# One iteration of an attention loop in another TensorE order: next queries unbroken, the last score block behind them, one projection moved

## The chip, the cores and the metric

The kernel runs on one core of one Trainium2 chip. Its five engines each work through a queue of their own: TensorE (PE, matrix products; its weight loads are listed as PEld), VectorE (DVE), ScalarE (ACT), GpSimd (POOL) and SyncE (SP, which here only issues DMA transfers). The metric is the time of one execution on the device in microseconds (us), and less is better.

## The reference

The kernel computes `x + ffn(attention(x))` in float32 with these steps:

- Attention over 16 sequences of 512 tokens with 512 features, 16 query heads of 64 features, and one key head and one value head that all query heads share. The input is normalised per token; `q = xn @ Wq / 8` and `k, v = xn @ Wkv`. The scores get a bias per head (given, 512 x 512), a causal mask and a mask of invalid keys, and one extra "null" key and value that every query may see. Softmax, the value product, an output product `out @ Wo` and a second normalisation follow.
- A routed feed-forward layer: an RMS norm, a router over 16 experts, the top 512 of 8192 tokens for each expert, two matrix products with a GELU between them, a share of each expert's result by its gate, and a scatter-add to the tokens.

Cut to the part that the change touches:

```
sim  = einsum('bhid,bjd->bhij', q, k) + bias      # scores
sim  = where(causal or masked, -big, sim)
attn = softmax(sim)
out  = einsum('bhij,bjd->bhid', attn, v)          # value product
out  = layernorm(out @ Wo) * g_out                # projection
```

## The kernel before, in words

The program has three stages: attention, the choice of tokens, and the experts. The change touches attention only.

**Tiling.** The loop `for p in range(B * HP + 1)` (L714) runs over pairs of heads: `B` = 16 sequences times `HP` = 8 pairs. `b` is the sequence and `hp` the pair in it. The 512 queries of a sequence are four blocks of 128. For causality block `q` needs only the first 128 * (q + 1) keys, so the four score blocks of one head are 128, 256, 384 and 512 columns wide.

**Software pipeline.** Four pairs are in work in one iteration. `now` is the pair whose scores are made and reduced. `ahead` is the next pair, whose queries are projected. `behind` is the pair before `now`: its probabilities are turned by DVE in 32 x 32 squares (`turn`, tile `sq`), and 16 DMAs (`move`: 10 issued by SP and 6 by POOL) put the squares in place (tile `pt`). `turned` is the pair before that, whose value product is made (`attend`, tile `ap`, copied by ACT to a tile `ot`, of which each sequence has 8). Beside these, the loop projects the sequence before with `Wo` (`second`, tile `op`) in the iterations hp = 1 to 7: a sequence has 8 pieces, 4 tiles of 128 tokens times 2 halves of the columns, and each piece is a sum over the 8 tiles `ot`, made in two steps of four products. It also normalises tiles of the sequence before (`OutNorm`) and of the sequence two ahead (`InNorm`), turns the next sequence's inputs (tile `xtp`, in `first`, hp = 0 to 3) and makes its keys and values (`kvs`, tile `kp`, hp = 2 and 4 in most sequences).

**What sets the order.** The order on each engine is the order in which the Python code calls it; nothing reorders it (`Pinned`, L121 to L138). The helpers `steps` and `some` split the generators: `queries()` stops after two of its four products, and `project()` stops after four of its eight. Each float32 product is two records of the profile.

**Products on PE.** Queries (`qp`), projection (`op`), keys and values (`kp`) and turns (`xtp`) use the array as a whole (128 rows by 128 columns in the profile's form "128*128"). Scores (`sp`) contract over 64 features and use the array's two row halves side by side ("64*128"); a bfloat16 product with `one_sb` (`sp<-km,one_sb`) puts the mask of keys in place first. The value product (`ap`) has 64 output columns per head and uses the two column halves side by side ("128*64").

**Buffers that tie the engines.** Score tiles have four PSUM buffers. `scores(3)` takes two, `scores(2, 0)` two, and `scores(1)` takes again the two that `scores(3)` had, so that it waits until DVE has reduced block 3 (`reduce`, which writes the minimum `nm`). The tile `sq` has one buffer: DVE may turn the next pair only when all 16 DMAs that read it have landed. PSUM tiles of queries, projection and value product rotate through three buffers (`ps_m`).

**Waits inside an iteration.** On DVE: reduce blocks 3, 2, 0; turn `behind`; what is left of the norms of the iteration before (`late`); reduce block 1; the first step of this iteration's norm (`n.a()`); sums; the second step (`n.b()`), which waits for a power that POOL computes (`lo_r`) in its queue behind its six DMA issues. On ACT: exponentials, the copy of the queries (`qa`), exponentials of block 1, the exponential of the null key (`ne`), the copy `ot`, then the normalising products. In iteration hp = 1 the projection needs, in its very last product, the eighth `ot` of the sequence before, which the same iteration's `attend` makes.

Of the kernel before, what the change touches and what calls it, by code (L numbers as in the profile page):

```python
# [26 lines left out]
def tile_adaln_ffn(  # L27
# [113 lines left out]
    with ExitStack() as st:  # L141
# [75 lines left out]
        def load_turned(hp):  # L217

            w = work.tile([P, DC, P], F32, name=f"wot_{hp}", tag="z" if hp % 4 < 2 else "xf")
            sy.dma_start(out=w, in_=wo_tc[:, :, hp * P : (hp + 1) * P])  # L220
            wots[hp] = w
# [17 lines left out]
        def router_column(hp):  # L239

            w = wots.pop(hp)
            wp = ps_m.tile([P, E], F32, name=f"wp_{hp}", tag="m")
            for c in range(DC):
                te.matmul(wp, w[:, c, :], rw_sb[:, c, :], start=(c == 0), stop=(c == DC - 1))
            se.copy(wo_sb[:, hp, D:], wp)
# [42 lines left out]
        def load_bias(p):  # L288

            b, hp = divmod(p, HP)  # L290
            bt = biasp.tile([P, 2, SW], F32, name=f"bias_{p}", tag="bias")
            sy.dma_start(out=bt, in_=causal[hp] if b > kept_in(hp) else bias[hp])
            return bt
# [5 lines left out]
        def mask_bias(p, bt):  # L299

            b, hp = divmod(p, HP)
            if b > kept_in(hp):
                return
            with tc.issue_after(ge.last.ins):
                for q in range(QB):
                    diag = bt[:, :, off[q] + ext[q] - P : off[q] + ext[q]]
                    ge.affine_select(
                        out=diag, in_=diag, pattern=[[0, 2], [-1, P]],
                        compare_op=ALU.is_ge, fill=-BIG, base=0, channel_multiplier=1,
                    )  # L310
            if b == kept_in(hp):
                ge.dma_start(out=causal[hp], in_=bt)
# [326 lines left out]
        def steps(*parts):  # L639
            for part in parts:  # L640
                if hasattr(part, "__next__"):
                    yield from part
                else:
                    part()
                yield

        def some(todo, n=None):

            while n is None or n > 0:
                if next(todo, todo) is todo:  # L650
                    return
                n = None if n is None else n - 1
# [39 lines left out]
        for pair in ((0, 1), (2, 3)):  # L692
            begun = [InNorm(seqs[0], t) for t in pair]
# [19 lines left out]
        now, behind, turned, late = None, None, None, ()  # L713
        for p in range(B * HP + 1):  # L714
            b, hp = divmod(p, HP)
            now, ahead = ahead, None
            if p + 1 < B * HP:
                if p > 0:
                    biases[p + 1] = load_bias(p + 1)
                ahead = Pair(seqs[(p + 1) // HP], (p + 1) % HP)  # L720
            bt = biases.pop(p, None)
            chains = [InNorm(seqs[c], t) for c, t in ins.get(p, ())]
            if p in norms:
                chains.append(OutNorm(seqs[norms[p][0]], norms[p][1]))
            second = steps(*[seqs[c].project(*divmod(h, 2)) for c, h in halves.get(p, ())])
            asked = ahead.queries() if ahead else steps()

            if now:
                now.scores(3)
                now.scores(2, 0)  # L730
                now.reduce(3, bt)
                now.exps(3)
                now.reduce(2, bt)
                now.reduce(0, bt)
                now.exps(2)
                now.exps(0)
            for n in late:
                n.root()
            if now and behind:
                behind.turn()  # L740
                behind.move(sy, range(6, SN * SN))
                behind.move(ge, range(6))
            for to, what in later.get(p, ()):
                sy.dma_start(out=to, in_=what)
            if 0 <= p - 2 < HP:
                load_turned(p - 2)
            if 0 <= p - HP < NT // P:
                rows = slice((p - HP) * P, (p - HP + 1) * P)
                sy.dma_start(out=out_t[rows, :], in_=x_t[rows, :])
            for c, t in loads.get(p, ()):  # L750
                seqs[c].load(t)
            for n in late:
                n.d()
                if isinstance(n, OutNorm):
                    n.route()
            some(asked, 1)
            if now:
                now.scores(1)
            else:
                seqs[end].project_part(2, range(early))  # L760
                behind.turn_last()
                seqs[end].project_part(3, range(early))
            some(asked)
            if now:
                now.reduce(1, bt)
                now.exps(1)
            some(second, 1)
            for n in chains:
                n.a()
            if p == 3:  # L770
                some(centered, 1)
            if now:
                now.sums()
            for part in kvs.get(p, ()):
                part()
            if p == 3:
                some(centered, 1)
            for c in {4: (0, 1)}.get(p, (p - 3,) if 4 < p < 3 + HP else ()):
                router_column(c)
            if turned:  # L780
                turned.attend()
            for n in chains:
                n.b()
            if p == 3:
                some(centered)
            if p + 1 < B * HP:
                mask_bias(p + 1, biases[p + 1])
            if now:
                now.normalize(0)
                now.normalize(3)  # L790
            for part in first.get(p, ()):
                part()
            if now:
                now.normalize(2, 1)
            some(second, 2)
            some(second)
            for n in chains:
                n.c()
            late = chains
            if HP - 2 <= p - end * HP < HP:  # L800
                seqs[end].project_part(p - end * HP - HP + 2, range(early))
            if not now:
                behind.attend()
            turned, behind = behind, now
# [505 lines left out]
    now = Expert(0, first)  # L1310
# [11 lines left out]
    for e in range(E):  # L1322
# [24 lines left out]
        if e == 0:  # L1347
# [10 lines left out]
            late = [part[3] for part in t]  # L1358
        else:
# [9 lines left out]
            late = []  # L1369
# [27 lines left out]
        now = nxt  # L1397
# [61 lines left out]
```

## Time and profile before

| what | value |
| --- | --- |
| median of 3 runs | 3511.76 us |
| lowest and highest | 3511.39 and 3514.19 us |
| the profiled execution's own time | 3511.39 us |
| its span (first to last instruction) | 3509.5 us |
| attention stage, roughly | 0 to 1840 us |
| choice of tokens | 1840 to 1990 us |
| experts | 1990 to 3509.5 us |
| PE busy in 500 to 1800 us | 1283.5 of 1300 us |

How to read it: the profile lists each engine's busy time, the granted TensorE clock in tenths, and the chain of work that ended last. A PE that reads busy is not one at its peak: the end of each product is modelled and overlaps the next product's start. What one product costs is therefore read from the distance between two starts. Attention takes about 110 us for each sequence in its steady part: the projections' long rows in the chain of waits repeat at 1001.14, 1110.77, 1223.99, 1334.09, 1443.09 and 1552.48 us.

### The profile page before, as it was taken

How to read it: one execution, taken by the hardware profiler on the slowest of the kernel's cores; microseconds unless marked ns; L12 is line 12 of the kernel's file. 1: busy time of each engine (PE TensorE's matmuls, PEld its weight loads, DVE VectorE, ACT ScalarE, POOL GpSimd, SP SyncE). 2: the span in 40 equal slices, each digit the busy share in tenths (PEclk: the TensorE clock that was granted, in tenths of full speed). 3: DMA queues.
4: the chain of work that ended last, by engine and by line, in shares of the span. 5: the costliest groups of instructions: out<-in, count | busy, mean ns of one | idle time of the engine just before them, and what ended most of it. 6: DMA issues, size and time to landing. Idle time of an engine off the chain costs nothing.

```text
span 3509.5 us, 50838 instructions
## 1 busy us (share of the span) xinstructions
PE 3352.9 (96%) x16100; PEld 2366.1 (67%) x16100; DVE 2342.2 (67%) x6089; ACT 1555.0 (44%) x4100; POOL 922.2 (26%) x1375
## 2 busy tenths in 40 slices
PE   7999999999999999999991899999999999999999
PEld 3555555555555555555550788888888888888887
DVE  6677777777777777776658865556556656655553
ACT  5676676677776777767640221111111211211111
POOL 3343333333333333333320222222111211222110
PEclk9999999999999999999995899999999999999999
DMA  6887877777776667667633244444333444444430
GB/s 218 272 254 241 254 227 230 219 242 229 231 233 204 209 216 216 207 209 214 197 112 110 83 144 129 134 127 127 107 102 122 139 135 131 132 127 127 135 101 12
DMA packets 272194, 601.33 MB, mean 171 GB/s; under 512 B 53032, under 2 KB 126424, under 8 KB 253496
## 3 DMA queue, kind: packets, MB, share of 16 engines
q1 hardware_dynamic: 213744, 467.72, 40.4%
q0 software_dynamic: 44272, 111.78, 13.5%
q10 hardware_dynamic: 13911, 18.60, 2.1%
q8 instruction: 129, 2.11, 0.2%
q14 instruction: 138, 1.12, 0.1%
HBM read 368.52 MB, written 61.87 MB: 123 GB/s over the span
## 4 chain that ended last, share of the span: by engine, by line
PE 81%; DVE 6%; issue 1%; SPq 1%; POOL 1%; DMA 1%; ACT 0%; DVEq 0%; POOLq 0%
PE op L131 11%; PE qp L131 10%; PE r_y L131 9%; PE sp L131 8%; PE pc L131 6%; PE pc_y L131 6%; PE pa_y L131 6%; PE pa L131 6%; PE ap L131 6%; PE pe L131 3%; PE pb L131 3%; PE pd L131 3%; DVE sq L131 2%; PE kp L131 1%; DVE p L131 1%
## 5 line engine op out<-in xcount | busy, mean ns | idle before, releaser
L131 DVE CUSTOM_DVE_ANT_0 p<-sp,bias,nn_sb 128x512 f32<-128x512 f32 (+3 forms) x1024 | 500.1, 544 | 256.8 <-PE sp L131 230.5
L131 ACT ACTIVATE p<-p,nm 128x512 f32<-128x512 f32 (+3 forms) x1024 | 561.8, 550 | 187.9 <-DVE nm L131 186.6
L131 POOL DMA_DIRECT2D pt<-sq x762 | 382.4, 508 | 840.8 <-issue 497.9
L131 PE MATMUL qp<-xnt,wq_sb 128*128 128x512 f32 x1024 | 514.7, 626 | 0.0
L131 PE MATMUL op<-wo_sb,ot 128*128 128x272 f32 (+1 forms) x1920 | 470.9, 391 | 4.3 <-ACT ot L131 4.3
L131 PEld LDWEIGHTS op<-wo_sb,ot 128*128 128x128 f32 x1920 | 357.8, 191 | 116.4 <-issue 55.0
L131 DVE STREAM_TRANSPOSE sq<-p 128x896 f32<-128x896 f32 x762 | 398.5, 587 | 24.1 <-DMA pt<-sq 10.1
L131 POOL DMA_INDIRECT out_dram<-y,tok x64 | 106.2, 1660 | 1151.7 <-ACT y L1278 1130.4
L131 ACT ACTIVATE p<-p,rs 128x512 f32<-128x512 f32 (+2 forms) x768 | 402.8, 603 | 1.3 <-DVE rs L131 1.3
L1186 ACT ACTIVATE h<-h,b_sb 128x512 f32<-128x512 f32 (+1 forms) x256 | 143.4, 607 | 526.6 <-DVE h L131 467.0
L131 PE MATMUL sp<-ka,qa 64*128 64x512 f32 (+3 forms) x2048 | 357.6, 440 | 1.6 <-ACT qa L131 1.6
L1278 ACT ACTIVATE y<-y,gg 128x512 f32<-128x512 f32 x64 | 46.2, 722 | 609.6 <-DVE y L131 411.1
L131 PE MATMUL ap<-pt,vp 128*64 128x512 f32 (+3 forms) x2048 | 310.1, 446 | 2.2 <-DMA x<-in_x_dram 1.2
L131 PEld LDWEIGHTS qp<-xnt,wq_sb 128*128 128x128 f32 x1024 | 175.4, 191 | 183.3 <-issue 167.8
L131 PEld LDWEIGHTS ap<-pt,vp 128*64 128x64 f32 x2048 | 138.0, 138 | 191.7 <-issue 159.6
L131 PE MATMUL pa<-xe,w 128*128 128x256 f32 x1024 | 243.6, 381 | 0.0
L131 PEld LDWEIGHTS sp<-ka,qa 64*128 64x128 f32 x2048 | 174.5, 190 | 86.0 <-issue 80.1
L131 PE MATMUL pa_y<-w,h 128*128 128x256 f32 x1024 | 231.5, 379 | 0.0
L131 PE MATMUL r_y<-w2t,hs 128*128 128x256 f32 x1024 | 231.5, 379 | 0.0
L131 PEld LDWEIGHTS pa<-xe,w 128*128 128x128 f32 x1024 | 195.6, 191 | 26.8
L131 PEld LDWEIGHTS r_y<-w2t,hs 128*128 128x128 f32 x1024 | 194.6, 190 | 26.5
L131 PEld LDWEIGHTS pa_y<-w,h 128*128 128x128 f32 x1024 | 194.6, 190 | 26.5
(201 smaller groups left out, 4959.5 us busy)
## 6 DMA issues: line engine op xcount, KB each, us to landing
bias<-causal SPq DMA_DIRECT2D x108, 1280.0 KB
w<-in_fc_dram SPq DMA_DIRECT2D x256, 512.0 KB
pt<-sq SPq DMA_DIRECT2D x1270, 80.0 KB
pt<-sq POOLq DMA_DIRECT2D x762, 80.0 KB
bias<-in_bias_dram SPq DMA_DIRECT2D x20, 1280.0 KB
x<-in_x_dram SPq DMA_DIRECT2D x64, 256.0 KB
out_dram<-in_x_dram SPq DMA_DIRECT2D x64, 256.0 KB
table<-xf SPq DMA_DIRECT2D x64, 256.0 KB
```

Source lines behind the costliest of these rows:

```text
L131: self.last = tc.keep_in_program_order(made(*args, **kwargs))
L1186: nc.scalar.activation(a[0], a[1], AF.Gelu, bias=b1_sb[:, self.e, f : f + 1])
L1278: nc.scalar.activation(y, y, AF.Copy, scale=self.gg[:, g, self.e : self.e + 1])
```

## The change

The loop's body is put in another order, in four points.

- The next pair's four query products stand in a row. Before, block 1's scores stood in the middle of them.
- Block 1's scores, and their reduction and exponentials, come behind the queries and behind the first half of the first projection piece. That first half (`some(second, 1)`) now stands ahead of the scores.
- In iterations hp = 1 that first half is not made there at all: the whole projection stands behind the value product.
- Where the iteration before left no norms (`late` is empty), the first step of this iteration's norms comes ahead of block 1. Otherwise it stays behind it.

No product, copy or transfer is added or removed.

```diff
-            some(asked, 1)
+            some(asked)
+
+            if hp != 1:
+                some(second, 1)
+            begun = () if late else chains
+            for n in begun:
+                n.a()
             if now:
                 now.scores(1)
+                now.reduce(1, bt)
+                now.exps(1)
             else:
                 seqs[end].project_part(2, range(early))
                 behind.turn_last()
                 seqs[end].project_part(3, range(early))
-            some(asked)
-            if now:
-                now.reduce(1, bt)
-                now.exps(1)
-            some(second, 1)
             for n in chains:
-                n.a()
+                if n not in begun:
+                    n.a()
...
-            some(second, 2)
             some(second)
```

## The prediction

> **What bounds the kernel now.** First the page, for the engine that carries the end:
>
> ```profile
> PE 3352.9 (96%) x16100; PEld 2366.1 (67%) x16100; DVE 2342.2 (67%) x6089; ACT 1555.0 (44%) x4100; POOL 922.2 (26%) x1375
> PE   7999999999999999999991899999999999999999
> PE 81%; DVE 6%; issue 1%; SPq 1%; POOL 1%; DMA 1%; ACT 0%; DVEq 0%; POOLq 0%
> ```
>
> PE carries 81% of the chain that ended last, and in attention (the first 21 slices) it reads nearly always busy. A gain must come from how closely its products follow each other, or from its few stalls. So next the timeline of PE through an ordinary iteration (hp = 3): start, length, product, records.
>
> ```profile
> 1187.18 1.98 PE L131 MATMUL qp<-xnt,wq_sb 128*128 128x512 f32 x4
> 1189.10 0.28 PE L131 MATMUL sp<-km,one_sb 64*128 64x256 bf16 x2
> 1189.22 0.60 PE L131 MATMUL sp<-ka,qa 64*128 64x256 f32 x4
> 1189.74 1.98 PE L131 MATMUL qp<-xnt,wq_sb 128*128 128x512 f32 x4
> 1191.56 1.89 PE L131 MATMUL op<-wo_sb,ot 128*128 128x256 f32 x8
> 1193.38 2.38 PE L131 MATMUL ap<-pt,vp 128*64 128x512 f32 x16
> 1195.69 0.66 PE L131 MATMUL xtp<-ident,xn 128*128 128x128 f32 x4
> 1196.18 1.89 PE L131 MATMUL op<-wo_sb,ot 128*128 128x256 f32 x8
> 1198.01 0.39 PE L131 MATMUL sp<-km,one_sb 64*128 64x512 bf16 x2
> ```
>
> Read the starts. Four query records take 1.92 us in front of scores and 1.82 in front of the projection; inside a row they follow at 0.429, 1.72 for four. So a row of whole-array products costs 0.10 more where it begins behind scores, and 0.10 more where it ends in front of scores or the value product; from queries to projection nothing is added. The value product's first two starts are 0.475 apart, later ones of its width 0.427: entry costs it 0.05, and its exit 0.10. Changing the form in which the array is used is what costs.
>
> Then who makes PE wait, and the timeline of all engines in an iteration hp = 1:
>
> ```profile
> PE sp L131 <- DVE nm L131: 21.8, 25, 4.5
> PE op L131 <- ACT ot L131: 4.3, 7, 1.0
> ```
> ```profile
> 1269.73 0.27 PE L131 MATMUL sp<-km,one_sb 64*128 64x256 bf16 x1 [0.29 <-DVE nm L131]
> ...
> 1272.36 3.15 DVE L131 STREAM_TRANSPOSE sq<-p 128x896 f32<-128x896 f32 x6 [1.00 <-DMA pt<-sq]
> ...
> 1278.53 0.67 ACT L131 ACTIVATE ot<-ap,nv_col 128x512 f32<-128x512 f32 x1
> ...
> 1279.25 0.70 PE L131 MATMUL op<-wo_sb,ot 128*128 128x256 f32 x2 [0.98 <-ACT ot L131]
> ```
>
> Block 1's scores wait for DVE, the transposes for the DMAs that read `sq`, and the projection's last product for the eighth `ot`. This chain, not PE, times hp = 0 and 1 together. Last, the windows (us from the start; PE busy; the number behind POOL is the granted clock):
>
> ```profile
> 600.91:604.32 3.41, 1.94 (x6) 0.72 (x5) 0.72 (x3) 1.52 (x4) 2.55 (x6) 1.00 0.73 204
> 604.32:607.73 3.41, 1.46 (x8) 0.72 (x8) 3.41 (x12) 2.03 (x6) 1.35 (x1) 1.00 0.82 241
> 607.73:611.14 3.41, 3.41 (x7) 1.66 (x6) 3.41 (x12) 2.67 (x11) 0.55 (x1) 0.50 0.83 324
> 1157.28:1160.69 3.41, 1.77 (x8) 0.88 (x8) 3.41 (x14) 2.34 (x7) 1.04 (x1) 1.00 1.02 368
> 1160.69:1164.10 3.41, 3.41 (x7) 1.91 (x6) 3.41 (x10) 2.36 (x9) 0.55 (x1) 0.50 0.22 90
> ```
>
> PE idle for 1.95 or 1.64 us of such a window is followed by one at half clock; idle for 1.47 us is not.
>
> **The change, part by part.** Every product, copy and DMA stays; PE's order changes, DVE's a little. SP's and POOL's queues keep theirs. The sum goes against the profiled execution: 3511.39 us, span 3509.5 and 1.9 around it. It is 0.4 below the median of 3511.76.
>
> *Queries in a row, scores behind the first half of the projection.* Before, from the first query to the end of the value product: 1.917 + 0.647 (scores) + 1.821 + 1.820 + 2.305 = 8.51 us by the starts. After: eight query records 1.821 + 4 x 0.429 = 3.537, projection 1.82 (the exit into scores costs what that into the value product did), scores 0.647, value product 2.305: 8.31. That is 0.20 less, if scores to value product costs 0.10 to leave and 0.05 to enter. The trace has no such pair. Bounds: nothing (then 0.34 is saved) and as much as the queries between them did (0.34, nothing saved). Nearest is value product to turned values, one part-array form to another: exit 0.10, exactly as into a whole-array product (both value products take 2.31 from start to start). So I take 0.15.
>
> By the Trainium skill, "TensorEngine Tiling (Array Packing)", Key Properties, changing the tiling mode drains the array; by that rule scores to value product is never free and the 0.34 falls away. No row here shows that pair.
>
> Where does it count? Not where keys and values, or the router's columns, stand between scores and value product, for they keep the same number of changes: hp = 2 and 4, and the iterations 3 to 10. Not in hp = 0 and 1, which the chain times. What is left: hp = 3, 5, 6, 7 of 14 sequences, three iterations of the last, one of the first: 60. 60 x 0.20 = 11.9 us, all on PE's path, since PE has no gap there.
>
> *Later scores of block 1.* They end up to 2.7 us later in an iteration. In hp = 3 DVE is free for them at 1192.17; they would be ready 8.3 us after the start of 1184.86, at about 1193.1. DVE so waits about 0.9 in hp = 2, 3 and 5, where `late` is short. It is hidden: DVE's first reduction of the next iteration waits 1.32 for its scores, and ACT's copy `ot` waits 1.44 for the value product, which stays in its place. Without that cover it is 0.9 x 3 x 14 = 38 us. Reduction 1 ends some 4 us before the next iteration's blocks 2 and 0 need its buffers.
>
> *Iteration hp = 1.* Block 1's scores come 0.86 us of queries later, so waits up to that size vanish: 0.3 to 0.9 in most sequences. The value product moves up by 1.73 (the half projection) and 0.2 to 0.4. Before, by the trace's landings, the last DMA landed 2.0 to 3.5 us ahead of it in the sequences without a long stall; so the value product now waits 0 to 1 us for that DMA. The late thing is then `ot`. Its chain is: reductions of hp = 0, transposes (end 1262.62), DMAs landed 1271.65, transposes 1272.36, norms, block 1, exponentials, `ot` 1278.53. Nothing in it moves, so where PE waited for `ot` (7 sequences) the iteration ends when it did: 0. PE only arrives earlier and waits 0.9 to 1.5 us instead of 0.2 to 1.0. In the four sequences with a stall over 2 us at block 1 (262.99, 381.02, 605.86, 1158.52) PE is last at the end: about 0.9 each, 3.6. In the rest with slack, three times 0.3: 0.9. Together 4.5.
>
> *The clock.* A wait of 0.9 to 1.5 us lies just below what halved the clock. I count one new half-clock window: 3.4 / 2 = 1.7 us lost. By the Trainium skill, "TensorE: Matmul & The Clock Gate", HAM oscillation, only idle gaps over some 3.4 us matter; by that rule no window is lost and the sum is 3495.0. The row at 1157.28 speaks against it: idle for 1.64 us, then half clock.
>
> *First norm step earlier* where `late` is empty: three or four iterations, DVE alone; 0, bounds -1 and +1.
>
> Sum: 3511.4 - 11.9 - 4.5 + 1.7 = 3496.7. I predict 3497.
>
> **The rivals.**
> - *Scores to value product is free:* 60 x 0.34 = 20.3 instead of 11.9: 3488. Against it the 0.10 of the nearest row. 0.08.
> - *It costs as much as what went:* the change does not do what it says, and only hp = 1 is left: 3508.6. For it, that every entry of a whole-array row costs 0.10 more than an exit; against it, the value product's 0.05. 0.12.
> - *The clock:* the longer wait for `ot` falls under half clock in all the 11 sequences that escape now: 11 x 1.7 = 18.7: 3513.7. It decides once idle time passes about 1.6 us in one window. 0.12.
> - *Slower:* block 1's lateness in hp = 2, 3 and 5 reaches PE. The place is DVE's reduction 1 and the norm, `ne`, `ot` and normalising behind it; the price 38 us: 3496.7 + 38 = 3535. It decides once the delay passes the 1.3 to 1.4 us of idle time that follow it; I work out 0.9. 0.12.
>
> **How the numbers follow.** The forecast holds 0.55 (own range 3491 to 3504); 0.01 is left for what I have not thought of. A measurement can tell about 0.2%, 7 us, from no change, so faster is below 3504.7: forecast, free switch and a little of the dear one's band, 0.66. Same: the two rivals near 3508 and 3514, 0.22. Slower: 0.12. Low end: the free switch, and three half-clock windows of now avoided, 3488 - 4 = 3484. High end: the clock, 3514. What is left out is mostly the slower case.
>
> **What would show it.** In PE's timeline: one row of 8 query records; starts of eight records 3.5 us apart from the projection's; the value product about 0.65 behind the scores. The long projection rows of two sequences 0.8 to 1 us closer than 109.6 to 110.3. The wait of scores for `nm` (21.8) down by half or more; that of the projection for `ot` (4.3) up to some 12; a new wait of the value product for `pt<-sq` of 1 to 4. It is wrong if the value product's first start lies over 0.8 behind the scores, if the clock shows 0.50 in most hp = 2, or if DVE's waits for `sp` reappear on PE.

## The result and the profile after

The changed kernel takes 3497.15 us (median of 6 runs, 3488.92 to 3498.16); the kernel before, timed beside it, 3511.57 us (6 runs). The ratio is 0.9951, with a 95% interval from 0.9939 to 0.9963; by the medians it is 14.4 us faster. The profiled execution of the change took 3488.92 us (span 3487.1) and is the lowest of its six; the profile of before took 3511.39. So the two traces differ by 22.4 us, 8 more than the medians. Where these 8 us are is the question of the first experiment.

The page of the changed kernel, for PE (engines, the PE slices, the chain that ended last):

```profile
PE 3325.6 (95%) x16100; PEld 2370.2 (68%) x16100; DVE 2348.1 (67%) x6089; ACT 1549.4 (44%) x4100; POOL 919.7 (26%) x1375
PE   7899999999999999999981999999999999999999
PE 81%; DVE 8%; DMA 4%; SPq 3%; issue 1%; POOL 1%; ACT 1%; DVEq 0%; POOLq 0%
```

The page hardly shows the gain. PE holds the same 81% of the chain; it is busy for 27.3 us less with the same 16,100 instructions. The timeline of PE in an ordinary iteration (hp = 3; start, length, product, records) does show it:

```profile
1279.55 3.70 PE L131 MATMUL qp<-xnt,wq_sb 128*128 128x512 f32 x8
1283.08 1.89 PE L131 MATMUL op<-wo_sb,ot 128*128 128x256 f32 x8
1284.90 0.28 PE L131 MATMUL sp<-km,one_sb 64*128 64x256 bf16 x2
1285.03 0.60 PE L131 MATMUL sp<-ka,qa 64*128 64x256 f32 x4
1285.55 2.38 PE L131 MATMUL ap<-pt,vp 128*64 128x512 f32 x16
1287.86 0.66 PE L131 MATMUL xtp<-ident,xn 128*128 128x128 f32 x4
1288.35 1.89 PE L131 MATMUL op<-wo_sb,ot 128*128 128x256 f32 x8
1290.17 0.39 PE L131 MATMUL sp<-km,one_sb 64*128 64x512 bf16 x2
```

From the first query to the turned values: 1287.86 - 1279.55 = 8.31 us, where before had 8.51. The value product starts 0.65 behind the scores' first product, and needs 2.31 to the next start, as before.

Now the waits of PE (total us, times, longest) and, of the timeline of all engines in an iteration hp = 1, its end:

```profile
PE op L131 <- ACT ot L131: 12.0, 12, 1.7
...
PE sp L131 <- DVE nm L131: 8.5, 11, 2.0
...
PE ap L131 <- DMA out_dram<-in_x_dram: 3.9, 2, 2.9
PE ap L131 <- DMA pt<-sq: 3.3, 4, 1.4
```
```profile
1254.63 3.15 DVE L131 STREAM_TRANSPOSE sq<-p 128x896 f32<-128x896 f32 x6 [0.22 <-DVE rms_t L131]
1254.69 2.38 PE L131 MATMUL ap<-pt,vp 128*64 128x512 f32 x16 [0.24 <-issue]
...
1259.19 0.51 ACT L131 ACTIVATE p<-p,nm 128x256 f32<-128x256 f32 x1 [2.66 <-DVE nm L131]
...
1260.79 0.67 ACT L131 ACTIVATE ot<-ap,nv_col 128x512 f32<-128x512 f32 x1
...
1261.51 0.70 PE L131 MATMUL op<-wo_sb,ot 128*128 128x256 f32 x2 [0.83 <-ACT ot L131]
```

The wait moved: block 1's scores wait 8.5 us for `nm` instead of 21.8, the projection 12.0 for `ot` instead of 4.3. The timeline says why `ot` is late. The value product is done by 1257.1, but its copy starts at 1260.79: it stands in ACT's queue behind block 1's exponentials, and these wait 2.66 us for DVE, which first turns the pair behind and ends the norms of the iteration before.

The spans of all profiles, cut at the starts of block 3's mask products (sums over sequences 2 to 14, in us against before; "ends" are sequences 0, 1 and 15; "behind attention" begins at about 1830 us before; "half clock" is the time in attention at a granted clock of 0.50). Each row is one execution. The profiles of the change, of rows only and of all three are the shortest of their runs, that of `ot` early with keys first is the longest of its six:

| kernel | hp 0, 1 | hp 2 | hp 3, 5, 6, 7 | hp 4 | ends | behind attention | span | half clock |
| --- | --- | --- | --- | --- | --- | --- | --- | --- |
| before, its own values | 333.4 | 197.4 | 723.8 | 191.0 | 384.0 | 1679.9 | 3509.5 | 44.4 |
| the change | -6.9 | -0.4 | -10.3 | 0.0 | -4.2 | -0.6 | -22.4 | 34.1 |
| the change again | -5.1 | +5.1 | -10.3 | 0.0 | -2.2 | +2.5 | -10.0 | 47.8 |
| rows only | -9.4 | +5.5 | 0.0 | 0.0 | -1.8 | +0.4 | -5.4 | 34.1 |
| hp = 1 only | -5.6 | +1.0 | 0.0 | 0.0 | +1.7 | +0.3 | -2.6 | 34.1 |
| without hp = 1 | -3.0 | +8.5 | -10.3 | 0.0 | -5.2 | +0.5 | -9.6 | 47.8 |
| `ot` early | -16.4 | +11.3 | -9.9 | 0.0 | -3.7 | +1.7 | -17.0 | 37.5 |
| `ot` early, without hp = 1 | -34.7 | +23.7 | -10.1 | 0.0 | -4.0 | +1.4 | -23.7 | 34.1 |
| keys first | -3.2 | -3.9 | -10.3 | -2.6 | -3.3 | +3.6 | -19.6 | 41.0 |
| `ot` early, keys first | -12.1 | -3.9 | -10.3 | -2.6 | -3.8 | +3.3 | -29.3 | 41.0 |
| all three | -34.4 | -1.0 | -10.3 | -2.6 | -4.3 | -5.1 | -57.7 | 30.7 |

### The profile page after: what moved, and what is told of

Read it like the earlier page. It is cut to its first block, busy times and chain, and to the rows that moved or that the text cites. A ratio compares the mean times of both kernels' runs of the same rounds, so it can differ in the third digit from the quotient of the medians.

```text
span 3487.1 us, 50838 instructions
## 1 busy us (share of the span) xinstructions
PE 3325.6 (95%) x16100; PEld 2370.2 (68%) x16100; DVE 2348.1 (67%) x6089; ACT 1549.4 (44%) x4100; POOL 919.7 (26%) x1375
## 4 chain that ended last, share of the span: by engine, by line
PE 81%; DVE 8%; DMA 4%; SPq 3%; issue 1%; POOL 1%; ACT 1%; DVEq 0%; POOLq 0%
PE op L131 11%; PE r_y L131 10%; PE qp L131 9%; PE sp L131 8%; PE pc L131 6%; PE pc_y L131 6%; PE pa_y L131 6%; PE ap L131 6%; PE pa L131 6%; PE pe L131 3%; PE pb L131 3%; PE pd L131 3%; SPq L131 3%; DVE sq L131 2%; PE kp L131 1%; DVE p L131 1%
## 5 line engine op out<-in xcount | busy, mean ns | idle before, releaser
L131 PE MATMUL qp<-xnt,wq_sb 128*128 128x512 f32 x1024 | 473.7, 605 | 0.0
L131 DVE STREAM_TRANSPOSE sq<-p 128x896 f32<-128x896 f32 x762 | 398.7, 589 | 25.8 <-DMA pt<-sq 10.2
L131 PE MATMUL ap<-pt,vp 128*64 128x512 f32 (+3 forms) x2048 | 315.0, 451 | 10.1 <-DMA out_dram<-in_x_dram 3.9
L131 PEld LDWEIGHTS qp<-xnt,wq_sb 128*128 128x128 f32 x1024 | 184.0, 189 | 199.2 <-issue 183.7
```

Source lines behind the costliest of these rows:

```text
L131: self.last = tc.keep_in_program_order(made(*args, **kwargs))
```

## The experiments

Each is an edit of the changed kernel, where nothing else is said. Each ratio is to the kernel before, timed beside it.

**The change again.** No edit. The question is how far the profiled execution stands for the kernel.

> The changed kernel once more, unchanged, to see how firm its time is: the profiled execution (3488.92 us) lies 8 us under the other five (3496.81 to 3498.16). If the 8 us are a matter of which long stalls and half-clock windows an execution meets, a new profile nearer 3497 us shows iterations hp = 3, 5, 6, 7 of the same 12.95, 16.61, 12.56 and 12.77 us, and the difference in hp = 0 and 1 and the first sequence. If the products' spacing itself differs, those four lengths differ.

Measured: 3501.29 us (9 runs, 3489.31 to 3506.84), ratio 0.9960 [0.9945, 0.9975]. Its profiled execution, 3501.29 us, is 12.4 longer than the first one. In the table hp = 3, 5, 6 and 7 and hp = 4 agree to 0.1 us; the difference is in hp = 0 to 2, in the ends, and 3.1 us behind attention, where the change does nothing. Of the 9.3 us in attention, half-clock time would account for (47.8 - 34.1) / 2 = 6.8; this is an estimate, which takes PE as busy all through it and as losing half of that time. The four lines are windows of this run (us from the start; length; then the busy time of PE, PEld, DVE, ACT and POOL; behind these the granted clock):

```profile
1040.50:1043.90 3.40, 1.73 (x10) 0.74 (x11) 3.40 (x14) 2.91 (x10) 0.84 (x2) 1.00 0.72 207
1043.92:1047.30 3.38, 3.38 (x16) 1.72 (x12) 3.35 (x9) 1.65 (x7) 0.40 (x2) 0.50 0.83 341
1159.90:1163.30 3.40, 1.72 (x9) 0.79 (x10) 2.37 (x10) 3.01 (x8) 2.20 (x5) 1.00 0.89 241
1163.32:1166.70 3.38, 3.38 (x19) 1.81 (x16) 3.34 (x13) 3.38 (x10) 0.00 (x0) 1.00 0.58 176
```

PE is idle for 1.67 us in the first window and 1.68 in the third; the clock halves behind the first and not behind the third. What follows: the saving by form changes is fixed, and that of hp = 0 to 2 is a matter of the execution, by several us.

**Rows only.** The kernel before with only its queries put in a row; block 1's scores come behind them, and the projection's first half stays behind the scores.

```diff
-            some(asked, 1)
+            some(asked)
             ...
                 now.scores(1)
             ...
-            some(asked)
```

> Queries in a row, scores of block 1 right behind them, the first half of the projection behind the scores as before. Theory of form changes: scores to projection brings a new entry (0.10) and the projection's exit into the value product (0.10 and 0.05) stays, so hp = 3, 5, 6, 7 keep their old lengths (13.14, 16.81, 12.75, 12.97) and nothing of the 11.9 us is gained; only the waits of block 1 in hp = 1 shrink: 3506 to 3511 us. Rival, an unbroken row of queries is worth it by itself: those iterations shorten by 0.2 us and the time is near 3498.

Measured: 3510.0 us, ratio 0.9996 [0.9986, 1.0006]: no difference. Its PE timeline in hp = 3:

```profile
1292.04 3.70 PE L131 MATMUL qp<-xnt,wq_sb 128*128 128x512 f32 x8
1295.67 0.28 PE L131 MATMUL sp<-km,one_sb 64*128 64x256 bf16 x2
1295.79 0.60 PE L131 MATMUL sp<-ka,qa 64*128 64x256 f32 x4
1296.32 1.99 PE L131 MATMUL op<-wo_sb,ot 128*128 128x256 f32 x8
1298.24 2.37 PE L131 MATMUL ap<-pt,vp 128*64 128x512 f32 x16
1300.55 0.66 PE L131 MATMUL xtp<-ident,xn 128*128 128x128 f32 x4
```

From the first query to the turned values 8.51 us, exactly as before. The queries in a row save nothing by themselves: the whole-array row is broken at another place, and the projection pays the entry behind the scores (1.92 between starts, 1.82 in the change). What pays in the change is the scores directly in front of the value product, which takes one change of form away. The waits do move here: block 1's scores wait 9.2 us for `nm` (21.8 before) and the projection 16.1 for `ot` (4.3 before). So the later scores of block 1 are enough to move that wait. Its profile has hp = 0 and 1 shorter by 9.4 us and hp = 2 longer by 5.5.

**hp = 1 only.** The kernel before, with only the projection of hp = 1 put entirely behind the value product.

```diff
-            some(second, 1)
+            if hp != 1:
+                some(second, 1)
...
-            some(second, 2)
```

> The kernel before with only the third point: in hp = 1 the projection entirely behind the value product. Theory: hp = 0 and 1 are timed by the chain of transposes, DMAs and the copy to ot, so PE only waits elsewhere: the wait of the projection for ot grows to 10 us or more, the sequences stay, 3509 to 3513 us. Rival: the projection's split is what cost, and hp = 1 shortens by 0.5 us or more in most sequences: 3503 or less.

Measured: 3512.1 us, ratio 0.9997 [0.9986, 1.0007]: no difference, though hp = 0 and 1 are 5.6 us shorter in its profile. The wait of scores for `nm` stays (23.0 us, 27 times). So this part alone doesn't touch block 1's wait. The wait for `ot` was expected to grow to 10 us or more, and that was wrong: it is 3.6 us (4.3 before). By the code the same products stand ahead of the last one of the projection as before, and block 1's wait stands ahead of them too, so PE comes to it no earlier.

**Without hp = 1.** The change with the projection of hp = 1 split as elsewhere.

```diff
-            if hp != 1:
-                some(second, 1)
+            some(second, 1)
```

> The changed kernel without its exception for hp = 1: there too the first half of the projection stands ahead of block 1's scores. Theory: the value product then comes 1.7 us later in hp = 1, so its waits for DMAs (about 9 us in all in the profile of the change) and those of block 1 for DVE (8.5 us) nearly vanish, PE arrives at the last product for ot when it did, and the iteration ends with the same chain: within 3 us of the changed kernel, or up to 5 us faster through fewer half-clock windows. Rival: the third point carries part of the gain; then 3500 us or more.

Measured: 3503.92 us, ratio 0.9975 [0.9964, 0.9985]; by the medians 2.6 us behind the change again, which was timed beside it, and the two intervals overlap. PE now waits longer for `ot`, as its waits say; below, its timeline at one of the two longest of these waits:

```profile
PE op L131 <- ACT ot L131: 25.4, 14, 3.4
```
```profile
1161.93 0.70 PE L131 MATMUL op<-wo_sb,ot 128*128 128x256 f32 x2 [3.38 <-ACT ot L131]
...
1162.79 1.66 PE L131 MATMUL sp<-ka,qa 64*128 64x512 f32 x4
```

The four scores records take 1.66 us where they take 1.02 at full clock (1262.37 in the changed kernel): the wait of 3.38 us is followed by half clock. This happens in five sequences, behind the five longest of these waits (267.52, 383.29, 606.01, 1049.36 and 1161.93; 1.95 to 3.40 us), and hp = 2 is 1.6 to 1.7 us longer in each of them, 8.3 us in all; the column has +8.5. So the exception of hp = 1 saves no work of PE. The `ot` arrives late either way; with the exception PE works in that time, its waits stay at 1.7 us and below, and the 12.0 of 25.4 us are left.

**`ot` early.** If the copy `ot` is late only by its place in ACT's queue, it should be called ahead of block 1's exponentials. In hp = 1 the value product is therefore called between block 1's reductions and its exponentials.

```diff
+            soon = hp == 1 and turned
             if now:
                 now.scores(1)
                 now.reduce(1, bt)
+                if soon:
+                    turned.attend()
                 now.exps(1)
...
-            if turned:
+            if turned and not soon:
                 turned.attend()
```

> The changed kernel with one thing more: in hp = 1 the value product's copy to ot stands ahead of block 1's exponentials in ACT's queue instead of behind them and the null key's. PE's order is the same. Theory: in the changed kernel hp = 1 ends when this copy does, and the copy waits not for the value product but for its turn behind DVE's reduction of block 1. Then the projection's waits for ot (9.6 to 12.0 us in two profiles) go to nearly 0, hp = 1 shortens by 0.7 to 1.7 us in most sequences, and the half-clock windows behind the longest waits go too: 8 to 12 us off, about 3490 us. Rival: DVE as a whole times hp = 0 to 2, and PE then waits at block 1 of hp = 2 for nm: as the changed kernel, 3498 to 3502.

Measured: 3495.62 us, ratio 0.9939 [0.9915, 0.9962]; the interval overlaps that of the change. No wait of the projection for `ot` is left, and hp = 0 and 1 are 9.5 us shorter than in the change. But hp = 2 gets 11.7 us longer: PE's turns wait 9.8 us for DVE's `vt`. The gain went to the next iteration. The 8 to 12 us expected off the change are not there: the time lies between the forecast (about 3490) and the rival (3498 to 3502), and what waits is `vt`, not block 1.

**`ot` early, without hp = 1.** Both edits. With `ot` on time, the exception has no late `ot` left to cover, and only delays what it puts behind.

> The same early copy to ot in the variant without the exception for hp = 1. Theory: with the copy early, the waits for ot (25.4 us there) go, and what the exception saved is no longer needed, while the value product no longer waits for DMAs: equal to the kernel with the exception and the early copy, or up to 3 us faster. If the exception is worth something by itself (block 1 earlier for DVE), this one is slower by 2 us or more.

Measured: 3486.6 us, ratio 0.9923 [0.9906, 0.9939]. That is 9.0 us below `ot` early, where 0 to 3 were expected; the two intervals overlap. The hp = 0 and 1 are 34.7 us shorter than before, and hp = 2 gives 23.7 of it back. Its waits, and its timeline in an iteration hp = 2:

```profile
PE xtp L131 <- DVE vt L131: 20.5, 10, 3.7
```
```profile
1163.41 3.15 DVE L131 STREAM_TRANSPOSE sq<-p 128x896 f32<-128x896 f32 x6 [1.18 <-DMA table<-xf]
...
1164.65 2.37 PE L131 MATMUL ap<-pt,vp 128*64 128x512 f32 x16
...
1166.85 0.48 DVE L131 CUSTOM_DVE_ANT_0 p<-sp,bias,nn_sb 128x256 f32<-128x256 f32 x1
...
1169.20 0.48 DVE L131 TENSOR_SCALAR vt<-kp,vk_col 64x256 f32<-64x256 f32 x1
...
1169.73 0.66 PE L131 MATMUL xtp<-ident,xn 128*128 128x128 f32 x4 [2.71 <-DVE vt L131]
```

The chain of transposes and DMAs no longer ends in hp = 1. Its lateness is carried on to hp = 2 by DVE's queue: transposes late by a DMA, then block 1, then the first norm step and the sums, then the copy `vt` of the values, whose products PE had issued before 1164.65.

**Keys first.** In the change, the keys and values of hp = 2 and 4 are called ahead of block 1's scores. So the scores stand directly in front of the value product there too, and DVE copies `vt` ahead of block 1.

```diff
+            for part in kvs.get(p, ()):
+                part()
             begun = () if late else chains
...
-            for part in kvs.get(p, ()):
-                part()
```

> The changed kernel with the keys' and values' products (hp = 2 and 4) ahead of block 1's scores instead of between them and the value product. Theory of form changes: hp = 2 and 4 now also lose one entry of a whole-array row, 0.20 us each, 28 times: 5.6 us off the changed kernel, hp = 4 at 14.49 instead of 14.69, about 3495. Rival, the lateness of block 1: its scores come another 1.8 us later, 2.7 us behind DVE in hp = 2; if DVE's idle time of 1.3 us is all the cover there is, PE waits in hp = 3 and 5 and the kernel is slower than the changed one by up to 20 us.

Measured: 3490.55 us, ratio 0.9931 [0.9913, 0.9948], where about 3495 us was expected. The iterations hp = 2 and 4 take 14.89 and 14.50 us by the median, where the change has 15.09 and 14.69. One change of form is worth the same 0.20 here; over 13 sequences 0.2 x 13 = 2.6, which the column hp 4 shows. The column of hp = 3, 5, 6 and 7 keeps its -10.3, so the rival of a later block 1 falls.

**`ot` early, keys first.** Both edits, with the exception of hp = 1.

> Both additions at once. If they are independent, the sum of both: about 14 to 17 us off the changed kernel, 3484 to 3487 us. If hp = 2 becomes timed by DVE once hp = 1 is shorter, less than the sum.

Measured: 3476.85 us, ratio 0.9893 [0.9875, 0.9910]. This is lower than the 3484 to 3487 us that the sum of both gave, so they are not independent: the wait for `vt` is gone from hp = 2 (-3.9 where `ot` early alone had +11.3), and hp = 0 and 1 keep 12.1.

**All three.** `ot` early, keys first, and no exception for hp = 1.

> The early copy to ot, the keys first, and no exception for hp = 1. In the variant with the early copy and no exception hp = 0 and 1 take 22.44 us instead of 23 to 28, but hp = 2 loses 24 us in all to waits of the turned inputs for DVE's vt and to half clock. Theory: the keys' products ahead of block 1 put vt ahead of block 1's reduction in DVE's queue, so these waits go: hp = 0 and 1 at 22.44 and hp = 2 at 14.89 together, 3486.6 less 27 less 2.6: 3457 to 3462 us. Rival: DVE cannot follow PE through hp = 0 to 2 at that pace and the waits move to block 1 of hp = 2 or to the transposes: no better than 3477.

Measured: 3456.58 us (4 runs, 3453.64 to 3457.59), before beside it 3505.83; ratio 0.9860 [0.9844, 0.9877]. It beats both kernels, and lies just below the 3457 to 3462 us expected. Its waits, and its timeline in an iteration hp = 1:

```profile
PE sp L131 <- DVE nm L131: 3.6, 5, 1.5
...
PE ap L131 <- DMA pt<-sq: 1.8, 2, 1.2
PE xtp L131 <- DVE vt L131: 1.5, 1, 1.5
```
```profile
1233.57 2.37 PE L131 MATMUL ap<-pt,vp 128*64 128x512 f32 x16
1235.88 0.66 PE L131 MATMUL xtp<-ident,xn 128*128 128x128 f32 x4
1236.00 0.69 ACT L131 ACTIVATE ot<-ap,nv_col 128x512 f32<-128x512 f32 x1 [2.00 <-PE ap L131]
...
1236.37 1.89 PE L131 MATMUL op<-wo_sb,ot 128*128 128x256 f32 x8
...
1238.19 0.39 PE L131 MATMUL sp<-km,one_sb 64*128 64x512 bf16 x2
```

ACT is at the copy before the value product is done, and the projection runs through. The hp = 0 and 1 together keep the -34.4 us, and hp = 2 no longer gives them back. Of the 57.7 us by the spans, 5.1 lie behind attention, where the edits do nothing.

## Why the prediction was right, point by point

The median came out 0.15 us from the 3497 forecast. That is closer than the steps deserve, and in part luck: the form changes are exact, the other steps are off by several us and partly cancel.

- **Queries in a row, scores behind the first half of the projection: right, to the hundredth.** The eight query records take 3.54 to the projection's start, the projection 1.82, scores 0.65, the value product 2.31, where I had worked out the same four. In each of hp = 3, 5, 6 and 7 the medians fall by 0.19 or 0.20, and the 52 iterations of sequences 2 to 14 by 10.3 us for the 10.4 worked out (52 x 0.20). The scores go over to the value product in 0.53 from their own first record, which is what they needed in front of queries; so leaving costs the same 0.10. Both rivals on this price fall. Rows only shows that the removed form change is the cause, not the row, and keys first takes away the same 0.20 at another place. The count of 60 was a little low: in the last sequence five iterations fell by 0.20 (hp = 0 and 2 to 5), not three, and hp = 0 of the others fell from 9.69 to 9.49 by the median.
- **Later scores of block 1: hidden as forecast, but not where I said on DVE.** DVE's timeline in that iteration hp = 3 of the changed kernel and behind it (the wait in brackets), and the second norm step of before:

```profile
1285.66 0.48 DVE L131 CUSTOM_DVE_ANT_0 p<-sp,bias,nn_sb 128x256 f32<-128x256 f32 x1 [1.04 <-PE sp L131]
...
1288.78 0.55 DVE L131 TENSOR_SCALAR z<-z,lo_mv,lo_r 128x512 f32<-128x512 f32 x1 [0.46 <-POOL lo_r L131]
...
1291.46 0.75 DVE L131 CUSTOM_DVE_ANT_0 p<-sp,bias,nn_sb 128x512 f32<-128x512 f32 x1 [1.14 <-PE sp L131]
```
```profile
1196.43 0.55 DVE L131 TENSOR_SCALAR z<-z,lo_mv,lo_r 128x512 f32<-128x512 f32 x1 [1.63 <-POOL lo_r L131]
```

  DVE waits 1.04 for block 1 (0.9 worked out). The next iteration's first reduction, which I named as the cover, still waits 1.14 (1.32 before) and gave up almost nothing. What took the delay on DVE is the wait for POOL's power `lo_r`: 1.63 before, 0.46 now. On ACT the forecast cover was used up: the copy `ot` waited 1.44 for the value product before, and 0.09 by the median in hp = 3 now. The iterations hp = 3 and 5 are shorter by the full 0.20. The slower rival falls.
- **Iteration hp = 1: the direction right, the sizes off.** `ot` takes the place of `nm` as the wait, in total 12.0 us as forecast ("up to some 12"), the longest 1.7 (1.5 forecast). For the gain of 4.5, hp = 0 and 1 measured 6.9 in the first profile and 5.1 in the second, both over 13 sequences, but not from the terms that I added. The four sequences with a long stall (2, 3, 5 and 10) gave 9.6 and 9.1 us, where I had 3.6; all half-clock time that sequences 2 to 14 had before lies in them. Sequence 7 lost 3.6 and 3.2, where I had nothing. The other eight moved by -1.7 to +2.0 us each and nearly cancel (-1.0 and +0.7 in sum), so "nothing in it moves" holds in the sum only. The value product's waits for DMAs I took as 0 to 1 us each; two of them sum to 3.9, one of 2.9, in sequence 7. What I left out is why the last link is late: it is a place in ACT's queue, and `ot` early moves it.
- **The clock: a sign that the execution decides.** I counted one new half-clock window, +1.7. In sequences 2 to 14, half-clock time was 20.5 us before; it is 10.2 in the first profile, three windows fewer, and again 20.5 in the second. By the same estimate that is -5.1 and 0. This time lies inside hp = 0 to 2, so it is not to be added to the row above: for both terms together I had -4.5 + 1.7 = -2.8, and hp = 0 to 2 measured -7.3 and 0.0. The point from which the rival was to decide, 1.6 us idle in a window, is no sharp point: windows with 1.67 us and with 1.68 us of idle time went both ways. The rival with all 11 sequences falls.
- **First norm step earlier: 0, not tried by itself.** Up to the end of sequence 0, 2.8 us are saved in the first profile and 1.0 in the second, where I had one iteration of 0.2. Which part does that stays open.

By the first profile the sum is 8 us too high (3496.7 against 3488.92), by the second 4.6 too low. The forecast hit the median because these executions lie around it. What is the same in both is the step of the form changes: 10.3 us in sequences 2 to 14.

## What to carry to other kernels

Count the changes of the array's form on PE's path, not the lengths of its rows: here each change removed between the scores and the value product is worth 0.20 us wherever PE has no gap; where a chain of other engines sets the time (hp = 1), two profiles do not show it apart from the rest. When a wait moves instead of going away, read which instruction the late one stands behind in its own engine's queue: two calls moved there (`ot` and the keys), with the exception of hp = 1 taken back, brought the ratio from 0.9951 to 0.9860, while `ot` alone could not be told from the change. Judge a change that works through waits by medians, since two profiles of the changed kernel differed by 12 us.

## What the runs showed of the hardware beyond what was expected

- The idle time at which the clock falls is a band, not one amount. These are windows of the changed kernel's first profile, columns as above:

```profile
600.20:603.60 3.40, 1.72 (x9) 0.93 (x9) 2.38 (x11) 2.67 (x8) 3.06 (x7) 1.00 0.84 209
603.62:607.03 3.41, 3.41 (x21) 1.79 (x20) 3.41 (x11) 3.41 (x9) 0.00 (x0) 1.00 0.71 205
811.90:815.31 3.41, 1.38 (x8) 0.32 (x6) 1.51 (x9) 3.41 (x13) 0.55 (x1) 0.99 0.48 147
815.31:818.72 3.41, 2.54 (x8) 1.01 (x10) 2.61 (x4) 0.04 (x1) 0.00 (x0) 0.50 0.97 298
```

  Idle for 1.68 us, then full clock; idle for 2.03 us, then half. In the profiles of all these kernels, between 150 and 1700 us, every such window that itself ran at full clock and had 1.95 us of idle time or more was followed by half clock, and none with 1.53 or less; between 1.54 and 1.93 both occurred. What decides there is open. Of the windows already at half clock, some with less idle time (0.31 to 1.30 us) were followed by another. By the Trainium skill, "TensorE: Matmul & The Clock Gate", HAM oscillation, it takes idle gaps of more than about 3.4 us; in the change again a window with 1.67 us of idle time in all was enough (1040.50), so for this kernel the measurement decides.
- Leaving the scores' form costs the same towards another part-array form as towards a whole-array product: the four scores records take 0.527 to 0.528 us to the value product's start in the changed kernel, and as much to the queries' start before (hp = 3, 5, 6 and 7, 52 iterations each). What the array does in the 0.10 us of this is not shown.
